# Inverse square roots computed with Newton's iteration on GpSimd instead of ScalarE's Sqrt, and the route exps of a row moved behind the exps of the band

## The chip, the cores and the metric

The kernel runs on one core of one Trainium2 chip. A core has five engines that run their own instruction queues in order and wait for each other through semaphores: TensorE (PE in the profile, with PEld for its weight loads), VectorE (DVE), ScalarE (ACT), GpSimd (POOL) and SyncE (SP, which here issues most of the DMAs). The metric is the device time of one execution in microseconds (us), as the median of several runs.

## The reference, cut to what matters

The program is two transformer-like layers on a float32 input x of shape (4, 512, 128): four batch rows of 512 tokens, 128 channels. In each layer the normalised input goes through an attention and through a mixture of experts, and both results are added to x.

```
def _layernorm(x, axis=-1, eps=1e-05):
    m = jnp.mean(x, axis=axis, keepdims=True)
    v = jnp.var(x, axis=axis, keepdims=True)
    return (x - m) / jnp.sqrt(v + eps)

# layer 0, attention: a window of 64 tokens, 16 heads
strain = disp_win - disp[:, :, :, None, :]
bond_act = gelu(strain @ W_strain + rel_emb @ W_pos)
damage = sigmoid(gelu(strain @ W_dmg + b_dmg) @ W_dmg_out + b_dmg_out)
logits = bond_act @ W_bond - 10.0 * damage
weights = softmax(where(cmask, logits, -inf))
out = einsum(weights, val_win) @ W_cproj

# layer 0, experts: 16, of which 4 are chosen for a token
t = x * rsqrt(mean(x * x, axis=-1) + EPS) * scale
g = einsum('bth,eh->bte', t, gate_w) + gate_b
vals, idx = top_k(g, 4);  w = softmax(vals)
# for each expert: acc + route * (swiglu(t @ w1 + b1) @ w2 + b2)

# layer 1: full attention (16 heads of 8), and 8 relu experts of which 2 are chosen
x = x + _L0_attn_ref(xn, ...) + _L0_ffn_ref(xn, ...)
xn = _layernorm(x)
x = x + _L1_attn_ref(xn, ...) + _L1_ffn_ref(xn, ...)
```

So there are two layernorms for each row, one per layer, and in layer 0 the experts' input t is the layernormed row divided once more by its root mean square. That makes three inverse square roots a row, each on 512 tokens (four tiles of 128, so a 128x4 tile), 12 in all.

## The kernel before

The four rows of the batch are called b = 0 to 3. A row's 512 tokens are four tiles of 128 partitions (TPB = 4). The code is written as Python generators, one for each job, and `weave` (L92) interleaves them: each track gets a number of steps, and the track that is furthest behind issues next. What the generators issue is then ordered by a scheduler that looks at readiness by its own estimates, so the order on an engine is near the woven order, not equal to it.

Jobs of layer 0, for a row b:

- `prepare(b)` (L492), with five yields: the layernorm of the row (xn), its transpose, the four projections `proj`, the division by the root mean square (sq, then tT after a transpose and the scale), the values, the gate scores, and the routes of the 16 experts with `routes` (L238) and `route_rows` (L264). The latter transposes the routes, copies them and stores them to DRAM with a DMA on SP (L275), from where each expert's row is loaded again, broadcast to all partitions (r8, L672).
- `band_logits(b)` (L543): the attention's logits, 64 steps. In each step VectorE subtracts two shifted views of `proj` into a tile z of 128x2048 elements (L560, both inputs in SBUF), ScalarE applies Gelu in place (L562 for the damage half, L566 twice for the bond half), and TensorE reduces z into a PSUM bank (L574). z comes from a pool of four buffers. At the end of the band two subtractions (L616) and two exps (L620) of 128x2048 follow, and their store to DRAM.
- `gated_experts(b)` (L647): the 16 experts, with Relu and Tanh on ScalarE, three instructions on VectorE each, and weights `wT` that are loaded from DRAM into two buffers.
- `band_values(b)` (L304): the weighted values of the attention, through DRAM to turn the band, and the output product.

For layer 1 there are `relu_experts(b)` (L392), which begins with the second layernorm and the routes of the 8 experts and adds up the experts' results on GpSimd (L447), and `full_attention` (L769).

The main loop (L719 to L734) weaves each band in two halves. In the first half the logits run with gated experts of this row, the values of the row before and the relu experts of the row before that. In the second half they run with the rest of the gated experts, with the relu experts of the row before, and with `prepare(b + 1)`, six steps. Row 0 is prepared ahead of the loop. After the fourth band, layer 1's attention runs with the last relu experts woven in.

`layernorm` (L207) takes mean and variance with bn_stats and bn_aggr on VectorE (L212, L215), calls `inv_sqrt` (L223), and forms xn with four instructions on VectorE (L218). `inv_sqrt` is a Sqrt on ScalarE (L226) with eps as bias and a reciprocal on VectorE (L228). For the root mean square VectorE squares the row (L510) and sums it (L512) before `inv_sqrt`. `routes` ranks the scores of a token by comparing all pairs (L248 to L254), takes an exp on ScalarE (L258), and normalises.

ScalarE holds one table of functions at a time. The trace shows an ACT_TABLE_LOAD ahead of the first Sqrt, Gelu or Exp after another of the three; Tanh needs one after Sqrt, and none after Gelu or Exp; Relu, copies and Identity need none.

Of the kernel before, what the change touches and what calls it, by code (L numbers as in the profile page):

```python
# [21 lines left out]

FP = mybir.dt.float32
AF = mybir.ActivationFunctionType
ALU = mybir.AluOpType
AX = mybir.AxisListType
PSUM = bass.MemoryType.PSUM

P = 128
B, T, C = 4, 512, 128  # L30
NT = B * T // P
TPB = T // P
# [59 lines left out]
def weave(*tracks):  # L92
    for _ in woven(*tracks):
        pass
# [3 lines left out]
def two_layers(ctx: ExitStack, tc: tile.TileContext, w: dict, consts: bass.AP, out: bass.AP):  # L98
# [26 lines left out]
    def c_(name):  # L125
        return cst[:, offs[name][0]:offs[name][1]]
# [41 lines left out]
    b2_1 = keep.tile([E1, C], FP, name="b2_1")  # L168
    nc.sync.dma_start(out=b2_1, in_=w["L1_ffn_b2"])

    eps = keep.tile([P, 1], FP, name="eps")
    nc.vector.memset(eps, EPS)
    top = keep.tile([P, 1], FP, name="top")
    nc.vector.memset(top, 0.5 * ALPHA * LIMIT)

# [28 lines left out]
    nc.scalar.copy(posb, pst[:, 0:WIN])  # L204


    def layernorm(b, dst, pin=False):  # L207

        mv = small.tile([P, TPB, 2], FP, tag="mv", name="mv")
        for i in range(TPB):  # L210
            st = small.tile([P, 6], FP, tag="st", name="st")
            ins = nc.vector.bn_stats(st, x1[:, b * TPB + i, :])  # L212
            if pin and not i:
                tc.keep_in_program_order(ins)
            nc.vector.bn_aggr(mv[:, i, :], st)  # L215
        rs = inv_sqrt(mv[:, :, 1], 1.0)
        for i in range(TPB):
            nc.vector.tensor_scalar(  # L218
                dst[:, i, :], x1[:, b * TPB + i, :], mv[:, i, 0:1], rs[:, i:i + 1],
                ALU.subtract, ALU.mult,  # L220
            )

    def inv_sqrt(src, scale):  # L223

        sd = small.tile([P, TPB], FP, tag="sd", name="sd")
        nc.scalar.activation(sd, src, AF.Sqrt, bias=eps, scale=scale)  # L226
        rs = small.tile([P, TPB], FP, tag="rs", name="rs")
        nc.vector.reciprocal(rs, sd)  # L228
        return rs

    def transposed(src):
# [3 lines left out]
            nc.tensor.transpose(pt[:, i * P:(i + 1) * P], src[:, i, :], ident)  # L235
        return pt

    def routes(pool, tag, g, n, k, less, dst):  # L238


        shape = [P, TPB, n, n]
        both = pool.tile([P, 2, TPB, n * n], FP, tag=tag, name="both")
        gt, eq = both[:, 0], both[:, 1]
        other = g[:, :, None, :].to_broadcast(shape)
        own = g[:, :, :, None].to_broadcast(shape)
        gt4 = gt.rearrange("p t (a b) -> p t a b", a=n)
        eq4 = eq.rearrange("p t (a b) -> p t a b", a=n)
        nc.vector.tensor_tensor(gt4, other, own, ALU.is_gt)  # L248
        nc.vector.tensor_tensor(eq4, other, own, ALU.is_equal)
        nc.vector.tensor_tensor(eq, eq, less[:, None, :].to_broadcast([P, TPB, n * n]), ALU.mult)  # L250
        nc.vector.tensor_tensor(gt, gt, eq, ALU.add)
        rank = small.tile([P, TPB, n], FP, tag=f"rank{n}", name="rank")
        nc.vector.tensor_reduce(rank, gt4, AX.X, ALU.add)
        nc.vector.tensor_scalar(rank, rank, float(k), None, ALU.is_lt)  # L254
        mx = small.tile([P, TPB], FP, tag="rmx", name="rmx")
        nc.vector.tensor_reduce(mx, g, AX.X, ALU.max)
        nc.vector.tensor_tensor(dst, g, mx[:, :, None].to_broadcast([P, TPB, n]), ALU.subtract)
        nc.scalar.activation(dst, dst, AF.Exp)  # L258
        nc.vector.tensor_tensor(dst, dst, rank, ALU.mult)
        nc.vector.tensor_reduce(mx, dst, AX.X, ALU.add)  # L260
        nc.vector.reciprocal(mx, mx)
        nc.vector.tensor_tensor(dst, dst, mx[:, :, None].to_broadcast([P, TPB, n]), ALU.mult)
# [195 lines left out]
    with ExitStack() as l0:  # L458
# [29 lines left out]
            nc.scalar.copy(merged[:, :, hg, :], pm[:, 0:2 * P].rearrange("p (k n) -> p k n", k=2))  # L488

        ready = {}  # L490

        def prepare(b):  # L492

            xn = prep.tile([P, TPB, C], FP, tag="xn", name="xn")
            layernorm(b, xn, b > 0)
            pt = transposed(xn)
            xnT = prep.tile([C, T], FP, tag="xnT", name="xnT")
            nc.scalar.copy(xnT, pt)
# [8 lines left out]
            ready[b] = [proj]  # L507
            yield
            sq = prep.tile([P, TPB, C], FP, tag="sq", name="sq")
            nc.vector.tensor_tensor(sq, xn, xn, ALU.mult)  # L510
            ss = small.tile([P, TPB], FP, tag="ss", name="ss")
            nc.vector.tensor_reduce(ss, sq, AX.X, ALU.add)  # L512
            rr = inv_sqrt(ss, 1.0 / C)
            for i in range(TPB):
                nc.vector.tensor_scalar_mul(sq[:, i, :], xn[:, i, :], rr[:, i:i + 1])

# [18 lines left out]
            )  # L535
            yield
            route = small.tile([P, TPB, E0], FP, tag="route0", name="route0")
            routes(zp, "z", scores, E0, K0, c_("lt16"), route)
            rT = route_rows(hold, route, E0, route_d[0][b], LIMIT + 1.0)
            ready[b] += [valn, tT, rT]  # L540
            yield
# [1 line left out]
        def band_logits(b):  # L543
# [70 lines left out]
            for half in range(2):  # L614
                e = zp.tile([P, 4, T], FP, tag="z", name="e")
                nc.vector.tensor_tensor(  # L616
                    e, logits[:, 4 * half:4 * half + 4, :],
                    pt[:, None, :].to_broadcast([P, 4, T]), ALU.subtract,
                )
                nc.scalar.activation(e, e, AF.Exp)  # L620
                nc.sync.dma_start(
                    out=by_t[0:P, 4 * half * T:(4 * half + 4) * T], in_=e.rearrange("p a t -> p (a t)")
                )
# [95 lines left out]
        for b in range(B):  # L719
# [9 lines left out]
            if b > 1:  # L729
                first.append((experts[b - 2], 21))  # L730
            if b + 1 < B:
                second.append((prepare(b + 1), 6))
            weave(*first)
            weave(*second)  # L734


    ctx1 = ctx.enter_context(ExitStack())
# [251 lines left out]
```

## Time and profile before

| what | value |
|---|---|
| median of 3 runs | 1378.02 us (1374.11 to 1379.18) |
| the profiled execution | 1381.3 us, its span 1379.5 us |
| mean granted TensorE clock | 0.941 of full speed |
| L560, subtractions z on VectorE | 256, 554.1 us |
| L562 and L566, Gelu on ScalarE | 128 and 256, 241.4 and 267.3 us |
| ACT_TABLE_LOAD on ScalarE | 43, 1283 ns each |
| Sqrt L226 on ScalarE | 12, 297 to 301 ns |
| reciprocal L228 on VectorE | 12, 164 to 178 ns |
| square L510 and sum L512 on VectorE | 4 each, 684 and 678 ns |
| addition L447 on GpSimd | 32, 1.26 to 9.51 us, median 1.28 |

The span is the time from the first to the last instruction of the profiled execution; the run's time lies 1.8 us above it. Busy times of different engines overlap, so they don't add up to the span. In the views that follow, a group's line gives its count, its busy time, the mean of one in ns, and the idle time of its engine just before it with what ended most of that. A timeline's line gives start and length in us. The order of the changed program's instructions on each engine is known too, without any time.

### The profile page before, as it was taken

How to read it: one execution, taken by the hardware profiler on the slowest of the kernel's cores; microseconds unless marked ns; L12 is line 12 of the kernel's file. 1: busy time of each engine (PE TensorE's matmuls, PEld its weight loads, DVE VectorE, ACT ScalarE, POOL GpSimd, SP SyncE). 2: the span in 40 equal slices, each digit the busy share in tenths (PEclk: the TensorE clock that was granted, in tenths of full speed). 3: DMA queues.
4: the chain of work that ended last, by engine and by line, in shares of the span. 5: the costliest groups of instructions: out<-in, count | busy, mean ns of one | idle time of the engine just before them, and what ended most of it. 6: DMA issues, size and time to landing. Idle time of an engine off the chain costs nothing.

```text
span 1379.5 us, 17426 instructions
## 1 busy us (share of the span) xinstructions
PE 1174.3 (85%) x6763; PEld 450.2 (33%) x6763; DVE 1012.4 (73%) x1085; ACT 1018.5 (74%) x1160; POOL 96.9 (7%) x68
## 2 busy tenths in 40 slices
PE   5676976678889789889989988887999899999997
PEld 2122323123433323353333334232333332333322
DVE  4999998999866999987799998843444434444451
ACT  4899997999968899988889988862454435545554
POOL 2000000000000002200002320012000000000000
PEclk9799998899879999999999999999999989999999
DMA  7121213446212445622244751235133200011100
GB/s 268 44 74 52 76 52 103 100 118 153 62 41 75 150 102 145 170 64 64 73 153 110 180 131 48 67 96 166 49 88 77 69 9 24 24 38 39 31 16 8
DMA packets 168524, 117.61 MB, mean 85 GB/s; under 512 B 66621, under 2 KB 149274, under 8 KB 166906
## 3 DMA queue, kind: packets, MB, share of 16 engines
q1 hardware_dynamic: 166970, 109.77, 29.3%
q0 software_dynamic: 1184, 6.29, 1.2%
q8 instruction: 54, 0.88, 0.3%
q10 hardware_dynamic: 288, 0.43, 0.1%
q14 instruction: 28, 0.23, 0.1%
HBM read 89.00 MB, written 27.46 MB: 84 GB/s over the span
## 4 chain that ended last, share of the span: by engine, by line
PE 59%; ACT 17%; DVE 13%; DMA 6%; issue 5%; SPq 0%; DVEq 0%; ACTq 0%
PE score L920 11%; PE lbank L574 10%; PE bank L381 8%; PE bank L442 7%; ACT z L566 6%; DVE z L560 5%; PE accbank L838 4%; ACT z L562 3%; PE gbank L674 3%; PE accbank L663 3%; DMA wb<-by_s 3%; PE gbank L681 2%; DMA wT<-wT_all 2%; DVE nmax L936 2%; PE abank L810 1%
## 5 line engine op out<-in xcount | busy, mean ns | idle before, releaser
L560 DVE TENSOR_TENSOR z<-proj 128x2044 f32<-128x2044 f32 (+31 forms) x256 | 554.1, 2189 | 29.0 <-PE lbank L574 12.6
L574 PE MATMUL lbank<-z,place 128*32 128x504 f32 (+18 forms) x2048 | 288.9, 639 | 110.1 <-ACT z L566 68.8
L936 DVE TENSOR_REDUCE nmax<-score 128x2 f32<-128x1024 f32 x128 | 156.3, 1225 | 182.3 <-PE score L920 180.1
L566 ACT ACTIVATE z<-z,posb 128x1024 f32<-128x1024 f32 (+31 forms) x256 | 267.3, 1097 | 10.2 <-DVE z L560 8.2
L942 ACT ACTIVATE ex<-score 128x1024 f32<-128x1024 f32 x128 | 130.3, 1023 | 159.7 <-PE score L920 159.7
L562 ACT ACTIVATE z<-z,brep 128x2048 f32<-128x2048 f32 (+31 forms) x128 | 241.4, 1906 | 5.3 <-DVE z L560 4.9
L920 PE MATMUL score<-k,q 32*128 32x512 f32 x512 | 152.2, 655 | 13.9 <-DVE nmax L936 11.7
L447 POOL TENSOR_TENSOR total<-total,part 128x512 f32<-128x512 f32 x32 | 82.6, 2580 | 1038.3 <-DVE part L446 1038.3
L920 PE MATMUL score<-qa,k 32*128 32x512 f32 x512 | 139.7, 648 | 2.1 <-ACT ex L942 2.1
L381 PE MATMUL bank<-xT,ew 128*128 128x512 f32 x256 | 136.2, 626 | 1.6 <-ACT h L389 0.8
L442 PE MATMUL bank<-h,ew 128*128 128x512 f32 x256 | 133.1, 619 | 4.7 <-issue 4.7
L389 ACT ACTIVATE h<-bank,cols 128x512 f32<-128x512 f32 x144 | 97.1, 684 | 45.3 <-PE bank L381 44.6
L574 PEld LDWEIGHTS lbank<-z,place 128*32 128x32 f32 x2048 | 43.0, 112 | 264.2 <-ACT z L566 143.9
L663 PEld LDWEIGHTS accbank<-wT,lin 128*128 128x128 f32 x512 | 72.2, 204 | 60.4 <-issue 34.6
L663 PE MATMUL accbank<-wT,lin 128*128 128x128 f32 x512 | 82.1, 297 | 10.1 <-DVE lin L661 10.1
L674 PE MATMUL gbank<-tT,wT 128*128 128x512 f32 x128 | 72.2, 647 | 17.4 <-DMA wT<-wT_all 16.5
L838 PE MATMUL accbank<-ex,vaug 128*32 128x512 f32 x512 | 70.8, 619 | 0.2 <-ACT ex L942 0.2
L681 PE MATMUL gbank<-tT,wT 128*128 128x512 f32 x128 | 70.6, 635 | 0.0
L920 PEld LDWEIGHTS score<-k,q 32*128 32x128 f32 x512 | 41.2, 187 | 89.0 <-ACT ex L942 44.1
L442 PEld LDWEIGHTS bank<-h,ew 128*128 128x128 f32 x256 | 44.2, 193 | 74.4 <-issue 71.0
L381 PEld LDWEIGHTS bank<-xT,ew 128*128 128x128 f32 x256 | 41.9, 192 | 72.8 <-issue 43.6
L659 DVE SCALAR_TENSOR_TENSOR lin<-lin,r 128x512 f32<-128x512 f32 x64 | 44.5, 695 | 28.6 <-ACT lin L683 28.3
(188 smaller groups left out, 1193.7 us busy)
## 6 DMA issues: line engine op xcount, KB each, us to landing
r<-route SPq DMA_DIRECT2D x96, 256.0 KB, 3.5
ew<-in_L_ffn_W SPq DMA_DIRECT2D x64, 256.0 KB, 3.4
wb<-by_s SPq DMA_DIRECT2D x32, 512.0 KB, 4.1
wT<-wT_all SPq DMA_DIRECT2D x48, 192.0 KB, 3.0
by_t<-e SPq DMA_DIRECT2D x8, 1024.0 KB
f<-by_t SPq DMA_DIRECT2D x128, 64.0 KB, 3.1
by_s<-g SPq DMA_DIRECT2D x16, 512.0 KB, 4.2
wb<-by_s SPq DMA_DIRECT2D x24, 256.0 KB, 3.6
```

Of the source, the lines that this page charges most:

```text
L381: mm = nc.tensor.matmul(ph, wt[:, c * P:(c + 1) * P], xT[:, b * T:(b + 1) * T], start=True, stop=True)
L442: nc.tensor.matmul(py, old[1][:, c, :], old[0][c], start=(c == 0), stop=(c == 3))
L560: nc.vector.tensor_tensor(z[:, :, :, 0:n], seen, own, ALU.subtract)
L562: nc.scalar.activation(z[:, :, :, 0:n], z[:, :, :, 0:n], AF.Gelu, bias=b_dmg)
L566: last = nc.scalar.activation(z[:, dq, :, 0:n], z[:, dq, :, 0:n], AF.Gelu, bias=posb[:, j:j + 1])
L574: mm = nc.tensor.matmul(ps[q:q + 32, t0:T], place[:, kind, 3 - dd:35 - dd], z[:, dq, hg, 0:n], start=(dd == 0), stop=(dd == 3),)
L663: nc.tensor.matmul(ya[:, i * P:(i + 1) * P], lin[:, i * P:(i + 1) * P], wT[:, 2, :], start=False, stop=(e == E0 - 1 and i == TPB - 1),)
L674: nc.tensor.matmul(pg, wT[:, 0, :], tT, start=True, stop=True)
L838: mm = nc.tensor.matmul(av[n][r:r + 32, :], vaug[b % 2][:, i, g * 4 + h, :], ex[n, i][:, h, :], start=(i == 0), stop=(i == TPB - 1),)
L920: mm = nc.tensor.matmul(ps[:, h - two, :], own[r, i * P:(i + 1) * P], seen[r, :], start=True, stop=True)
L936: freed.append(nc.vector.tensor_reduce(nmax[n % 2][:, i, two:two + 2, 8:9], ps, AX.X, ALU.max, negate=True))
L942: freed.append(nc.scalar.activation(ex[n, i][:, two:two + 2, :], ps, AF.Exp, scale=inv))
```

## The change

1. `inv_sqrt` no longer uses ScalarE. It adds eps to the variance, takes a first guess from the float's bits (shift right by one on VectorE, then 0x5F3759DF minus that), and improves it with three Newton steps of four instructions each. All but the shift run on the engine `on`: GpSimd, or VectorE for row 0's layernorm.
2. The root mean square of xn is taken from the variance that the layernorm already has: the mean of xn squared is var times rs squared, two instructions on GpSimd in place of a square and a sum over the row on VectorE.
3. `prepare(b + 1)` gets four steps instead of six in the second half of the band, and what is left of it (the routes and their rows) is issued after that half. The exp of these routes gets a high priority and a dependency without a semaphore that places it behind the band's last exp, `exps[-1]`.

In the changed program the instructions of one inverse root stand on GpSimd as an addition, then, after VectorE's shift, 13 instructions of which each waits for the one before. For the 11 roots that are not row 0's layernorm VectorE's next user (xn or sq) waits for the last of them. In VectorE's order there is nothing between shift and sq for row 0's root mean square and nothing between shift and xn for the last layernorm; elsewhere there are between 2.4 and 4 us of instructions. The routes of rows 1 to 3 stand behind the band's two subtractions for the exps, and their later instructions between the first z of the next band. ScalarE's order holds 17 table loads.

```diff
-    eps = keep.tile([P, 1], FP, name="eps")
-    nc.vector.memset(eps, EPS)
...
-    def layernorm(b, dst, pin=False):
+    def layernorm(b, dst, pin=False, on=nc.gpsimd):
...
-        rs = inv_sqrt(mv[:, :, 1], 1.0)
+        rs = inv_sqrt(mv[:, :, 1], on)
...
+        return mv[:, :, 1], rs
...
-    def inv_sqrt(src, scale):
-        sd = small.tile([P, TPB], FP, tag="sd", name="sd")
-        nc.scalar.activation(sd, src, AF.Sqrt, bias=eps, scale=scale)
+    def inv_sqrt(src, on=nc.gpsimd):
+        v = small.tile([P, TPB], FP, tag="sd", name="sd")
+        on.tensor_scalar(v, src, EPS, None, ALU.add)
+        guess = small.tile([P, TPB], I32, tag="guess", name="guess")
+        nc.vector.tensor_scalar(guess, v.bitcast(I32), 1, None, ALU.logical_shift_right)
         rs = small.tile([P, TPB], FP, tag="rs", name="rs")
-        nc.vector.reciprocal(rs, sd)
+        on.tensor_scalar(rs.bitcast(I32), guess, -1.0, float(0x5F3759DF), ALU.mult, ALU.add)
+        for _ in range(3):
+            a = small.tile([P, TPB], FP, tag="newton", name="newton")
+            on.tensor_tensor(a, rs, rs, ALU.mult)
+            on.tensor_tensor(a, a, v, ALU.mult)
+            on.tensor_scalar(a, a, -0.5, 1.5, ALU.mult, ALU.add)
+            on.tensor_tensor(rs, rs, a, ALU.mult)
         return rs
...
-    def routes(pool, tag, g, n, k, less, dst):
+    def routes(pool, tag, g, n, k, less, dst, behind=None):
...
-        nc.scalar.activation(dst, dst, AF.Exp)
+        with tc.high_priority(offset=4000 if behind else 0):
+            exp = nc.scalar.activation(dst, dst, AF.Exp)
+        if behind:
+            tc.add_manual_dep(
+                exp.ins, behind.ins.name,
+                mybir.DependencyInfo(mybir.DependencyClass.NoSync, mybir.DependencyReason.DATA),
+                reason="one table for both",
+            )
...
-            layernorm(b, xn, b > 0)
+            var, rs = layernorm(b, xn, b > 0, nc.gpsimd if b else nc.vector)
...
-            nc.vector.tensor_tensor(sq, xn, xn, ALU.mult)
-            ss = small.tile([P, TPB], FP, tag="ss", name="ss")
-            nc.vector.tensor_reduce(ss, sq, AX.X, ALU.add)
-            rr = inv_sqrt(ss, 1.0 / C)
+            ms = small.tile([P, TPB], FP, tag="ss", name="ss")
+            nc.gpsimd.tensor_tensor(ms, rs, rs, ALU.mult)
+            nc.gpsimd.tensor_tensor(ms, ms, var, ALU.mult)
+            rr = inv_sqrt(ms)
...
-            routes(zp, "z", scores, E0, K0, c_("lt16"), route)
+            routes(zp, "z", scores, E0, K0, c_("lt16"), route, exps[-1] if exps else None)
...
-                nc.scalar.activation(e, e, AF.Exp)
+                exps.append(nc.scalar.activation(e, e, AF.Exp))
...
-                second.append((prepare(b + 1), 6))
+                preparation = prepare(b + 1)
+                second.append((preparation, 4))
             weave(*first)
             weave(*second)
+            for _ in preparation:
+                pass
```

More of the change, by code (lines that the diff above doesn't have):

```diff
@@ L23 @@
 FP = mybir.dt.float32
+I32 = mybir.dt.int32
 AF = mybir.ActivationFunctionType
@@ L490, in two_layers @@
         ready = {}
+        exps = []
         def prepare(b):
             xn = prep.tile([P, TPB, C], FP, tag="xn", name="xn")
-            layernorm(b, xn, b > 0)
+            var, rs = layernorm(b, xn, b > 0, nc.gpsimd if b else nc.vector)
             pt = transposed(xn)
```

## The prediction

> **What bounds the kernel now.** I read the page first: busy shares and the 40 slices. VectorE (DVE) and ScalarE (ACT) have nearly the same busy time, and both are near nine tenths up to slice 26 (about 900 us), where the last band ends; afterwards PE alone is full.
>
> ```profile
> PE 1174.3 (85%) x6763; PEld 450.2 (33%) x6763; DVE 1012.4 (73%) x1085; ACT 1018.5 (74%) x1160; POOL 96.9 (7%) x68
> DVE  4999998999866999987799998843444434444451
> ACT  4899997999968899988889988862454435545554
> ```
>
> A share over the whole span hides that a band has two halves, so I cut the span at the band ends and at the start of each next row's preparation, and then into shorter stretches (columns after the times: PE, PEld, DVE, ACT, POOL busy with counts, granted clock, DMA).
>
> ```profile
> 133.00:235.00 102.00, 77.18 (x420) 30.92 (x420) 95.52 (x104) 91.12 (x113) 0.11 (x1) 0.88 0.20 61
> 235.00:355.00 120.00, 88.42 (x720) 33.22 (x720) 116.17 (x98) 114.48 (x113) 0.00 (x0) 0.91 0.50 127
> 355.00:470.00 115.00, 102.42 (x422) 43.38 (x423) 84.60 (x119) 90.35 (x109) 4.30 (x4) 0.88 0.24 67
> 600.00:705.00 105.00, 94.72 (x428) 43.23 (x427) 85.37 (x128) 88.14 (x108) 4.19 (x3) 0.95 0.25 75
> ```
>
> ```profile
> 199.00:221.00 22.00, 15.42 (x88) 5.04 (x80) 17.52 (x22) 19.87 (x26) 0.11 (x1) 0.84 0.11 34
> 436.00:456.00 20.00, 16.57 (x76) 7.44 (x75) 18.71 (x24) 16.12 (x21) 1.38 (x2) 1.00 0.30 75
> 671.00:691.00 20.00, 17.15 (x76) 8.15 (x76) 19.68 (x24) 16.45 (x22) 1.70 (x2) 0.91 0.21 66
> ```
>
> First halves (235 to 355) are bound by DVE and ACT together, 97% and 95%. Second halves (355 to 470, 600 to 705) are bound by PE's in-order queue, with ACT only 79 and 84% busy. Inside them one stretch of 20 us belongs to DVE: that of the routes (L248 to L262).
>
> Next, the table loads, by shape, and then those that lie on the chain of waits that ended last (start, length, engine, line; a load has no tile).
>
> ```profile
> L226 ACT ACT_TABLE_LOAD x11 | 14.1, 1283 | 2.0 <-issue 1.8
> L566 ACT ACT_TABLE_LOAD x11 | 14.1, 1283 | 0.2
> L258 ACT ACT_TABLE_LOAD x7 | 9.0, 1283 | 0.1
> ```
>
> ```profile
> 171.10 1.28 ACT L562
> 366.95 1.28 ACT L679
> 610.52 1.28 ACT L566
> 1112.13 1.28 ACT L226
> ```
>
> All seven groups add to 43 loads, 55.2 us of ACT. Only nine are on the chain: these four, and those at 26.98, 232.80, 237.82, 467.55 and 701.82.
>
> Last, GpSimd (POOL), which gets the new work. Its one arithmetic instruction, L447, takes 1.27 us when VectorE runs reductions from PSUM, and 9.50 us when four z subtractions (both inputs in SBUF) run back to back:
>
> ```profile
> 528.40 9.50 POOL L447 TENSOR_TENSOR total<-total,part 128x512 f32<-128x512 f32 x1 [19.49 <-DVE part L446]
> ```
>
> ```profile
> 528.24 8.53 DVE L560 TENSOR_TENSOR z<-proj 128x1976 f32<-128x1976 f32 x4
> ```
>
> **The change, part by part.** All sums are against the profiled span of 1379.5 (its run: 1381.3, 3.3 above the median of 1378.0); I put the difference on the median.
>
> A. *ACT relief.* The changed program's instruction order has 17 table loads: the first (hidden under the input's load, as now), then Gelu, Exp, Gelu in band 0 and four per later band (a pair around each relu route, one Exp and one Gelu at each band's end). 26 fewer x 1.283 = 33.4 us, and 12 square roots x 0.298 = 3.6 us. By place: 6 go in 133 to 235, 9 in 355 to 470, 7 in 600 to 705, 2 in 835 to 930, 2 at 1112. On the chain are the four shown, 5.1 us, and the root at 1113.42, 0.31: **-5.4**. The others (22 loads, 11 roots: 31.5 us) are off it; between 0 and half of that, since 16 of the loads lie in halves where ACT idles 17 to 25 us. Two of PE's waits for a Gelu stand right behind such loads, 5.3 us at 136 and 4.8 at 210; I take half of these, **-5**.
> The row says 1.283 and nothing more: the load at 133.30 starts where the tanh ends (132.64 + 0.64), and its root starts at 134.59. The Trainium skill ("ScalarE: Activation LUTs", What ACT_TABLE_LOAD costs) counts some 2.66 us for a switch, a drain included; 26 would be 69 us, and this trace has no such gap.
>
> B. *Routes of the next row moved behind the band's exps.* What leaves the second half: in the three short stretches the next engine is ACT (19.87 less two loads = 17.3 of 22), PE (16.57 of 20) and PE (17.15 of 20), so at best -4.7 - 3.4 - 2.9 = -11. What comes at the band's end: now from the first subtraction for the exps (L616) to the next band's first Gelu it takes 11.0, 9.7 and 9.7 us (228.08 to 239.12, 464.79 to 474.44, 699.05 to 708.71). After, VectorE has two of these, 4.48, the scores, 0.23, five instructions of the routes before the first z, 4.9 (36.97 to 41.87 in band 0, the same order), and a z, 2.28: 11.9, so +0.9, +2.2, +2.2; and rank (1.21) with five small ones (some 0.2 each) between the next z, in a half where VectorE is 97% busy: +2.2 x 3. Cost 0 to 11.9, taken as 10: **-1**, ends -11 and +12. The moved DMA (L275, the routes' store) goes on SP behind the band's stores and 9 to 13 loads of f; behind it stand the last two f, the r8 loads and wb, which the first expert needs only after its matmul. The weave (6 to 4) also spreads the preparation: by the 32nd z of a band six gated experts have begun instead of five. In 395 to 436 and 640 to 671 PE is 100% busy, and an expert costs it 1.0 + 1.0 + 1.2 = 3.2; in the first half it costs VectorE and ACT 2.1 each: 2 x (2.1 - 3.2) = **-2.2**.
>
> C. *Newton on POOL.* Per inverse root: an addition, a shift on VectorE (which waits for POOL), then 13 dependent POOL instructions on 128x4, then VectorE's xn or sq, which wait; behind these in VectorE's queue are the z, and behind those ACT and PE. On POOL, L447's additions for the experts queue behind. No row shows a 128x4 arithmetic instruction here. Nearest: POOL's memset of 128x16, 0.11 us, below; above, 0.4, a third of L447's 1.27 with its 128 times longer rows. I take 0.2, nearer the small one. While z run, the chain hardly moves (the 9.50), so what VectorE has between is no cover: once it reaches its wait it stands for the chain, 13 x 0.2 = 2.6. Four of the 11 POOL sites are on VectorE's chain:
> - band 0's second root: shift and sq follow each other behind the fourth z (33.8): 2.6 + sq 0.9 + transposes 0.66 + tT 0.67 + L530 1.06 and handoffs give scores at 39.8 instead of 36.64: +3.2;
> - row 1's layernorm at 127 to 140, where the chain is VectorE throughout: 2.6 less three steps gained beside L592: +2.0;
> - the two layernorms at 601 to 606, on VectorE: +2.4;
> - the last one, in attention: 15 steps, 3.2, against 0.64 now (1113.33 to 1113.97): +2.6.
> **+10.2** in all, 54 p - 0.6 for a step of p. The other seven lie where VectorE idles 20 to 30 us per half: 0, at most 2 each. Ends: +5.3 (p = 0.11) and +35 (p = 0.4, and 14).
> What speaks against the change is the Trainium skill ("SBUF — State Buffer", Who interferes with whom): a VectorE instruction with two SBUF inputs and a GpSimd instruction that reads SBUF exclude each other for the whole instruction. With a z of 2.19 before each step a chain would last 28 us, four of them 114; the rows agree on the blocking, but VectorE's own wait ends it.
>
> D. *RMS from the variance.* L510 (0.68) and L512 (0.68) go, four times; about one and a half of these pairs lie where VectorE is the chain (0.66 at 11.11; row 1): **-2**. Band 0's first root moves onto VectorE, 14 small steps at 6.4 to 9, covered by the wait for w_pos to 9.8; without that cover it would cost 1.5.
>
> Sum: -5.4 - 5 - 1 - 2.2 + 10.2 - 2 = **-5.4**, so 1378.0 - 5.4 = 1372.6, said as 1372.
>
> **Rivals.**
> - *ACT was the limit wherever a load stood.* For it: DVE and ACT are equal in sum, and the loads come in clusters (seven in 355 to 385). Against: ACT idles in those halves. Price: half of the 31.5 us instead of 5, and a step of 0.11: -5.4 - 15.7 - 1 - 2.2 + 5.3 - 2 = -21: 1357.
> - *POOL's chain takes the loads' place.* Slower: the step is 0.4, and half of each hidden stall shows. For it: the 9.50 us, and each step waits for the one before. Against: memsets follow each other within 0.1. -15.6 + 35 = +19: 1397. It decides from 54 p - 0.6 = 15.6, p = 0.3.
> - *The routes don't fit at the band's end.* B at +12: 1385. For it: VectorE 97% busy there. Against: ACT must go through the exps and two loads there anyway.
>
> **How the numbers follow.** Forecast 0.46 (own range 1362 to 1381), ACT 0.24, POOL 0.19, routes 0.11. A measurement tells some 0.5% from no change, 1371.1 to 1384.9. Faster: 0.21 of the forecast and 0.24 = 0.45. Same: 0.25, and 0.02 and 0.03 of the last two = 0.30. Slower: 0.17 + 0.08 = 0.25. The range, 1352 to 1394, leaves out the ends of ACT's and POOL's cases.
>
> **What would show it.** Right: 17 loads; POOL steps of some 0.2 us; VectorE waiting 2 to 3 us for POOL at xn and sq; the stretch of the routes gone from the second half; scores of band 0 near 40. Wrong: steps over 0.3 us or POOL waits in VectorE's list above 30 us; second halves shorter by over 10 us each; a first half longer by over 5 us.

## The result, and the profile after

The changed kernel takes 1399.15 us (median of five runs, 1398.56 to 1400.96), the kernel before in the same session 1378.02 (1374.11 to 1379.18): a ratio of 1.0165, 95% interval 1.0147 to 1.0184. It is slower by some 22 us, where 1372 was forecast with a range to 1394. Its profiled execution has a span of 1396.8 us, 17.3 more than that of before.

The page's busy times, and the slices of the engines that changed:

```profile
PE 1180.0 (84%) x6763; PEld 449.9 (32%) x6763; DVE 1007.3 (72%) x1090; ACT 983.0 (70%) x1122; POOL 161.5 (12%) x230
DVE  4899888999796899979679997873444444445451
ACT  4799796889797699979769996963354425555554
POOL 2000110000301013421001331002000000000000
```

ScalarE has 35 us less to do, VectorE 5 less, and yet the span is longer. So on these two the time went into waiting. POOL has 65 us more, but is busy for only 12%: no engine has become full. PE's busy time is 5.7 us longer for the same 6763 matmuls, at a mean granted clock of 0.930 where before had 0.941; whether that matters is taken up with the iterations below.

The table loads are the 17 that the program's order promised (line, engine, operation, count, busy us, ns of one, idle time before):

```profile
L580 ACT ACT_TABLE_LOAD x5 | 6.4, 1283 | 0.1
L268 ACT ACT_TABLE_LOAD x4 | 5.1, 1283 | 0.1
L638 ACT ACT_TABLE_LOAD x4 | 5.1, 1283 | 0.1
L584 ACT ACT_TABLE_LOAD x3 | 3.8, 1283 | 0.1
L179 ACT ACT_TABLE_LOAD x1 | 1.3, 1283 | 1.7 <-PEq L995 1.7
```

The list of VectorE's waits has a kind that was not there before (who waits, for whom, us in all, times, the longest):

```profile
DVE xn L217 <- POOL rs L237: 21.5, 7, 3.7
DVE sq L533 <- POOL rs L237: 10.0, 3, 3.7
```

Ten waits, 31.5 us. One of them in the timeline, VectorE and POOL together (start, length, and in brackets the idle time before and its releaser):

```profile
414.92 0.16 DVE L229 TENSOR_SCALAR guess<-sd 128x4 int32<-128x4 int32 x1
414.99 0.68 DVE L536 TENSOR_TENSOR x<-x,xn 128x512 f32<-128x512 f32 x1
415.16 0.56 POOL L231 TENSOR_SCALAR rs<-guess 128x4 int32<-128x4 int32 x1 [36.28 <-DVE guess L229]
415.59 2.04 DVE L578 TENSOR_TENSOR z<-proj 128x1820 f32<-128x1820 f32 x1
415.81 1.89 POOL L234 TENSOR_TENSOR newton<-rs 128x4 f32<-128x4 f32 x1
417.77 0.20 POOL L235 TENSOR_TENSOR newton<-newton,sd 128x4 f32<-128x4 f32 x1
418.06 0.19 POOL L236 TENSOR_SCALAR newton<-newton 128x4 f32<-128x4 f32 x1
418.34 0.20 POOL L237 TENSOR_TENSOR rs<-rs,newton 128x4 f32<-128x4 f32 x1
...
420.57 0.20 POOL L237 TENSOR_TENSOR rs<-rs,newton 128x4 f32<-128x4 f32 x1
420.81 0.87 DVE L533 TENSOR_SCALAR sq<-xn,rs 128x128 f32<-128x128 f32 x4 [3.17 <-POOL rs L237]
421.59 2.04 DVE L578 TENSOR_TENSOR z<-proj 128x1816 f32<-128x1816 f32 x1
```

Three things are to be seen. A step is 0.20 us long, but the next one starts 0.28 after it (417.77, 418.06, 418.34). While VectorE's z runs (415.59 to 417.63), POOL gets one step through, which takes 1.89 and ends 0.07 after the z; the step before it (415.16) is stretched in the same way beside VectorE's addition x, to 0.56 us. And then VectorE stands for the rest of the chain, with its next z (421.59) behind sq in its queue.

Last, a band's end, where the routes have been put (VectorE, from the subtraction for the exps to the next band's first z):

```profile
459.57 4.49 DVE L634 TENSOR_TENSOR e<-logits,bank 128x2048 f32<-128x2048 f32 x2 [0.21 <-PE bank L244]
467.92 0.69 DVE L462 TENSOR_TENSOR part<-bank,r 128x512 f32<-128x512 f32 x1 [3.87 <-issue]
470.67 0.22 DVE L550 TENSOR_TENSOR scores<-bank,gate_b 128x64 f32<-128x64 f32 x1 [2.05 <-PE bank L548]
470.92 1.23 DVE L257 TENSOR_TENSOR both<-scores 128x1024 f32<-128x1024 f32 x1
...
475.73 2.28 DVE L578 TENSOR_TENSOR z<-proj 128x2048 f32<-128x2048 f32 x1
```

The scores come 11 us after the first subtraction, and the first z 16. From that subtraction to the next band's first Gelu it takes 14.9, 18.5 and 20.2 us, 53.6 together, against 30.4 before. So after this reading there were two suspects: POOL's chains (31.5 us of waits) and the band's end (23 us longer).

### The profile page after: what moved, and what is told of

It reads as the page before. It is cut to its first block, busy times and chain, and to the rows that moved or that the text cites. A ratio compares the mean times of both kernels' runs of the same rounds, so it can differ in the third digit from the quotient of the medians.

```text
span 1396.8 us, 17551 instructions
## 1 busy us (share of the span) xinstructions
PE 1180.0 (84%) x6763; PEld 449.9 (32%) x6763; DVE 1007.3 (72%) x1090; ACT 983.0 (70%) x1122; POOL 161.5 (12%) x230
## 3 DMA queue, kind: packets, MB, share of 16 engines
q1 hardware_dynamic: 166970, 109.77, 29.4%
## 4 chain that ended last, share of the span: by engine, by line
PE 55%; DVE 18%; ACT 12%; issue 8%; DMA 5%; POOL 2%; SPq 1%; DVEq 0%
PE score L941 10%; PE lbank L592 8%; PE bank L397 8%; DVE z L578 8%; PE bank L458 6%; ACT z L584 4%; PE accbank L859 4%; ACT z L580 3%; PE gbank L692 3%; PE gbank L699 2%; PE accbank L681 2%; DVE nmax L957 2%; DMA wb<-by_s 2%; PE bank L244 1%; PE abank L813 1%
## 5 line engine op out<-in xcount | busy, mean ns | idle before, releaser
L592 PE MATMUL lbank<-z,place 128*32 128x504 f32 (+18 forms) x2048 | 289.8, 640 | 102.2 <-ACT z L580 55.8
L463 POOL TENSOR_TENSOR total<-total,part 128x512 f32<-128x512 f32 x32 | 93.5, 2920 | 712.1 <-DVE part L462 712.1
L692 PE MATMUL gbank<-tT,wT 128*128 128x512 f32 x128 | 76.9, 685 | 8.1 <-DMA wT<-wT_all 8.1
L699 PE MATMUL gbank<-tT,wT 128*128 128x512 f32 x128 | 70.8, 636 | 0.0
L695 ACT ACTIVATE glu<-gbank,gbt 128x512 f32<-128x512 f32 x64 | 43.7, 684 | 23.7 <-PE gbank L692 23.5
```

What stands on the lines that cost most here:

```text
L592: mm = nc.tensor.matmul(ps[q:q + 32, t0:T], place[:, kind, 3 - dd:35 - dd], z[:, dq, hg, 0:n], start=(dd == 0), stop=(dd == 3),)
L692: nc.tensor.matmul(pg, wT[:, 0, :], tT, start=True, stop=True)
```

## The experiments

Times are medians. The experiments were timed in groups, each with its own runs of the kernel before (medians 1375.4 to 1378.0); each ratio is to the kernel before of the same group. Where medians and ratios of two groups give different differences, both are said. A table of progress helps: the start of VectorE's z number n (from 0; 64 of them to a band, 256 in all) in the profiled executions, worked out from the traces, as us later than in the kernel before.

```
n      before   after   one_iter  five_iter  row0_dve  no_sqrt
8        52.1    +4.1      +0.7      +4.7      -6.0      -3.6
64      232.5    +9.8      +2.3     +11.7      -1.7      +2.9
128     469.2    +6.5      -5.6     +16.6      -6.8     -10.9
192     703.4   +15.0      -4.0     +36.1      +1.8     -12.4
255     893.9   +22.4      +2.3     +46.5      +9.4     -14.7
```

### Undoing one part each

Newton on VectorE at every root, the routes still at the band's end:

```diff
-    def inv_sqrt(src, on=nc.gpsimd):
+    def inv_sqrt(src, on=nc.vector):
...
-            nc.gpsimd.tensor_tensor(ms, rs, rs, ALU.mult)
+            nc.vector.tensor_tensor(ms, rs, rs, ALU.mult)
```

> Every root's Newton steps (and the mean square) on VectorE; the routes stay behind the band's exps. Theory POOL (the 31.5 us that VectorE waits for POOL at xn and sq are the loss): VectorE does 14 small steps of some 0.1 to 0.2 itself, 2 to 3 us a root in place of 3.2 to 3.7, and is no longer slowed by anything on POOL: 10 to 20 us less than the changed kernel, 1379 to 1389. Theory END (the loss is the way from the first subtraction for the exps to the next band's first Gelu, 14.9 + 18.5 + 20.2 = 53.6 us after against 30.4 before, 23.2 more): those three transitions stay at 50 us or more, and the time at 1390 or more.

1395.65 us, ratio 1.0131 (1.0096 to 1.0166). Only 3.5 to 4.7 below the changed kernel, with transitions of 52.3 us, so END seemed to hold.

The routes back in the second half, Newton still on POOL:

```diff
-                preparation = prepare(b + 1)
-                second.append((preparation, 4))
+                second.append((prepare(b + 1), 6))
...
-            for _ in preparation:
-                pass
...
-            routes(zp, "z", scores, E0, K0, c_("lt16"), route, exps[-1] if exps else None)
+            routes(zp, "z", scores, E0, K0, c_("lt16"), route)
```

> The routes back in the second half (the preparation spread over six steps, no wait for the band's exps); Newton on POOL and the RMS from the variance stay; 23 table loads. Theory POOL: VectorE's waits for POOL stay near 30 us and the time at 1390 or more. Theory END: transitions back near 30 us, 23 us less, of which the six table loads that come back and the routes' place in the second half take 0 to 10 again: 1376 to 1386.

1405.05 us, ratio 1.0196 (1.0158 to 1.0234): slower still, with transitions of 11.3, 9.7 and 8.5, 29.4 us together, as short as before. VectorE's waits for POOL are 33.1 us. END in its simple form is gone, and POOL's forecast for this run held.

The roots by Sqrt again, the rest of the change kept:

```diff
-        on.tensor_scalar(v, src, EPS, None, ALU.add)
...
+        nc.scalar.activation(sd, src, AF.Sqrt, bias=eps, scale=1.0)
+        nc.vector.reciprocal(rs, sd)
```

> The roots back on ScalarE (Sqrt and VectorE's reciprocal, 38 table loads); routes behind the band's exps and the RMS from the variance stay. Theory POOL: 31.5 us of waits gone, some 10 to 15 of them given back to ScalarE's table loads: 1378 to 1389. Theory END: transitions stay at 50 us or more, the time at 1392 or more.

1402.84 us, ratio 1.0170 (1.0113 to 1.0227), in END's interval; the next experiments show that it was for another reason in part.

Newton on VectorE and the routes back, that is, both of the above:

> Both undone: Newton on VectorE, the routes back in the second half; what is left of the change is roots without a table and the RMS from the variance (23 table loads for 43). Theory POOL: as the first run less a few us, 1375 to 1389. Theory END: below the run with Newton on POOL and the routes back by what VectorE saves, 1368 to 1380, and 20 us or more below the first run.

1390.14 us, ratio 1.0094 (1.0062 to 1.0125). Neither theory: POOL plays no part here, the band's end neither, 20 of the 43 loads are gone, and it is still 14 us slower than before. So Newton's steps seem to cost time on VectorE too (the run with the first guess alone, below, shows it), and POOL's are 15 us dearer (1405 against 1390).

### Each part alone

The loads alone, by leaving the root out:

```diff
-        nc.scalar.activation(sd, src, AF.Sqrt, bias=eps, scale=scale)
+        nc.scalar.activation(sd, src, AF.Identity, bias=eps, scale=scale)
```

> The kernel before with the 12 square roots left out (ScalarE writes variance plus eps with the function Identity, which is in every table; the reciprocal follows): 23 table loads instead of 43, nothing put in their place, routes where they were. This part of the computation is left out. It is the whole of what the change can get from the roots' loads. Theory RELIEF (the loads cost what the forecast said, some 8 of its 10.4 us for these 20 loads, and the loss comes from what replaces them): 1364 to 1372. Rival NOTHING (ScalarE's loads lie in its idle time, the order that the scheduler makes around them matters more): 1373 to 1382. Rival LIMIT (ScalarE was the bound at each load): 1350 to 1360.

1365.21 us, ratio 0.9918 (0.9889 to 0.9948): RELIEF. 20 loads are worth 10 to 11 us, 0.5 each of their 1.283.

The routes' move alone (the diff of the run with the routes back, the other way round, on the kernel before):

> The kernel before with the move of the routes alone: preparation spread over four steps, the routes issued after the second half, their exps behind the band's; the roots by Sqrt and the RMS from the squares as before (some 36 loads). Theory END (the move costs about 23 us at the three transitions and wins back less in the second halves): 1388 to 1400. Rival POOL (the move is worth about nothing, as the forecast's -1 with 7 loads fewer): 1368 to 1380.

1390.21 us, ratio 1.0112 (1.0060 to 1.0164). END's number, 15 us slower than before in spite of seven loads fewer.

Both:

> The last two together: square roots left out (this part of the computation is not done) and the routes moved; 17 table loads as in the changed kernel, no Newton, the RMS from the squares. Theory END: 15 us or more above the run without square roots and with the routes in place, 1380 to 1395. Rival POOL: within 5 us of that run or below, 1360 to 1375; then what the changed kernel loses is Newton's, 25 us or more.

1370.27 us, ratio 0.9962 (0.9928 to 0.9997). This run has the changed kernel's 17 loads and its routes, and no Newton. The changed kernel is 28 us above it (1.0165 - 0.9962 = 0.0203 of 1378); by the two intervals it is 21 to 35 us. With no roots in the way, moving the routes costs about 5 us, hardly more than the runs scatter; beside Sqrt it costs 15, and beside Newton on POOL it gains 4 to 6 (1.0196 to 1.0165, or 1405 to 1399).

The preparation earlier, the routes at the band's end as in the changed kernel:

```diff
-                second.append((preparation, 4))
+                second.append((itertools.islice(preparation, 4), 6))
```

> The changed kernel with the four steps of the next row's preparation at the first four of six places of the second half, as before, instead of the four spread over all of it; the routes stay behind the exps. If the lateness of the preparation (scores at 470.7, 11 us after the first subtraction for the exps) makes the transitions long: scores are ready before the exps, the three transitions fall from 53.6 to 40 to 45 us, the time to 1385 to 1392. If the routes' own 5 us on VectorE and the loads do: transitions of 50 us or more, time within 5 us of 1399.

1397.06 us, ratio 1.0158 (1.0094 to 1.0221), though the transitions are now 9.0, 10.6 and 10.6 us, 30.2 together: the 23 us are gone from the band's end and the time is the same. A likely reason, not measured, is that in the long band's end work was done that otherwise is done in the halves beside it. The forecast here was right in its mechanism (the lateness makes the transitions long) and wrong in its price.

### What a step costs

Fewer steps, in the changed kernel:

```diff
-        for _ in range(3):
+        for _ in range(1):
```

> The changed kernel with one Newton iteration instead of three; two iterations of each root are left out. 8 dependent POOL steps fewer at each root. Theory STEPS (VectorE stands for the whole chain at every site, on the time's path: 10 sites x 8 x 0.28 = 22 us, plus what the slowed steps took): 1372 to 1382, VectorE's waits for POOL down from 31.5 to some 10 us. Rival CROSSING (the cost lies in the order and the two crossings between VectorE and POOL, which stay): 1390 to 1398.

1376.01 us, ratio 0.9981 (0.9958 to 1.0005): 23 to 25 us less for 8 steps at 11 roots, 0.26 to 0.29 a step. Its list of VectorE's waits for POOL:

```profile
DVE xn L217 <- POOL rs L237: 7.2, 7, 1.4
DVE sq L533 <- POOL rs L237: 3.3, 3, 1.4
```

10.5 us instead of 31.5. As much left the time as left the waits. The sites that the prediction put on VectorE's chain (its list of four, of which the third is two layernorms, so five of the ten waits) gave up 10.7 us of waits, the other five 10.3. Had only the first group been on the path, half of the gain would have come off.

More steps, range(5):

> The changed kernel with five iterations instead of three: eight POOL steps more at each root. If each step stands on the time's path at the same price: 1399 + 23 = 1422, 1415 to 1428, and VectorE's waits for POOL up from 31.5 to some 53 us. If a part of the waits is hidden from some length on or there is a threshold: 1400 to 1412, or over 1435.

1428.70 us, ratio 1.0362 (1.0330 to 1.0394): 27 to 30 more, at or just above the upper end of the 1415 to 1428 expected, and the waits up to 55.8:

```profile
DVE xn L217 <- POOL rs L237: 35.3, 7, 5.7
DVE sq L533 <- POOL rs L237: 20.5, 4, 5.9
```

No threshold shows: the price is 0.26 to 0.29 us a step from one iteration to three, and 0.31 to 0.34 from three to five. The eleventh root, row 1's second one, which the z covered with three iterations, comes out as a wait too.

Whether the waits merely went along with the loss, or are it, can be read from VectorE's own time up to the end of the last z (us, worked out from the profiled executions, one of each kernel):

```
                       before  no_sqrt  one_iter   after  five_iter  row0_dve
to the end of z 255     896.0    881.2     898.3   918.4      942.5     905.4
busy                    796.8    796.2     791.2   792.7      792.6     794.8
idle, for POOL            0.0      0.0       9.5    28.3       51.2      24.3
idle, all else           99.2     85.1      97.5    97.3       98.6      86.3
```

From one iteration to three and to five the stretch grows by 20.1 and 24.1 us, the waits for POOL by 18.8 and 22.9, and all other idle time stays within 1.3 us. So the waits were added to the idle time and not taken out of it. This also bears on a rival that no run holds fixed, the granted TensorE clock: it is 0.945 with one iteration, 0.930 with three and 0.923 with five, and PE's busy time for the same matmuls is 1166.1, 1180.0 and 1184.0 us. Had the slower PE made VectorE wait longer for the others, the last row would have grown with it.

The second group can be seen by itself in band 1, from z 64 to z 128, where only three of its waits stand (368, 378 and 421 us). With one iteration these waits are 5.9 us shorter and the stretch 4.6; with five they are 7.4 longer and the stretch 8.2. Place by place the match is not always so good: with five iterations band 0 has 6.6 us more of waits and is 1.9 longer.

The same on VectorE: the run of 1390 (Newton there, routes in place) with range(0), the first guess alone.

> The run with Newton on VectorE and the routes in place (1390), all three iterations left out: each root is its first guess, three small VectorE instructions in place of fifteen, values within some 3 per cent of the true ones; 23 loads. If VectorE's steps cost what they did there (25 us for 13 more of them at 12 sites, 0.16 us each): 1390 - 12 x 12 x 0.16 = 1367, 1362 to 1372. If not the steps but the data or the order made the runs without square roots fast: 1376 to 1390.

1365.12 us, ratio 0.9900 (0.9863 to 0.9936): 25 to 27 us for 144 steps, 0.17 to 0.19 each. VectorE's own steps are 0.16 long and start 0.20 apart, so nearly all of their time shows too.

### The other two places

The squares back (the RMS as before, its root on POOL):

```diff
-            nc.gpsimd.tensor_tensor(ms, rs, rs, ALU.mult)
-            nc.gpsimd.tensor_tensor(ms, ms, var, ALU.mult)
-            rr = inv_sqrt(ms)
+            nc.vector.tensor_tensor(sq, xn, xn, ALU.mult)
...
+            nc.vector.tensor_reduce(ss, sq, AX.X, ALU.add)
+            rr = inv_sqrt(ss, nc.gpsimd, 1.0 / C)
```

> The changed kernel with the RMS from the squares again (two VectorE instructions of 0.68 us, four times), its root still on POOL; 17 loads. If the mean square from the variance costs (the run with Sqrt, routes moved and the mean square on POOL was 12.6 us above the one without it): 1386 to 1394. If it gives the 2 us of the forecast: 1399 to 1404.

1398.78 us, ratio 1.0123 (1.0073 to 1.0173). This lies just below the range for a gain and well above that for a cost. Its runs spread from 1390.6 to 1401.2; by the medians the part costs nothing, by the ratios 6 us. A gain of 2 us is unlikely by the intervals, and not excluded by these four runs.

Row 0's second root on VectorE:

```diff
-            nc.gpsimd.tensor_tensor(ms, rs, rs, ALU.mult)
...
+            on = nc.gpsimd if b else nc.vector
+            on.tensor_tensor(ms, rs, rs, ALU.mult)
...
+            rr = inv_sqrt(ms, on)
```

> The changed kernel with row 0's second root on VectorE too, where VectorE stood idle for 11.98 us ahead of the first z; in the changed kernel the shift waits behind four z. If that place is what band 0 pays: scores of band 0 near 31 instead of 40.7, the eighth z 6 to 8 us earlier, and the time 1390 to 1394. If the later waits swallow it: 1396 to 1400.

1389.49 us, ratio 1.0086 (1.0052 to 1.0119): 10 us back from one root. The reason stands in VectorE's timeline. First the changed kernel:

```profile
11.03 0.69 DVE L536 TENSOR_TENSOR x<-x,xn 128x512 f32<-128x512 f32 x1
23.71 2.29 DVE L578 TENSOR_TENSOR z<-proj 128x2048 f32<-128x2048 f32 x1 [11.98 <-ACT proj L523]
...
33.76 0.16 DVE L229 TENSOR_SCALAR guess<-sd 128x4 int32<-128x4 int32 x1
37.59 0.88 DVE L533 TENSOR_SCALAR sq<-xn,rs 128x128 f32<-128x128 f32 x4 [3.67 <-POOL rs L237]
40.73 0.22 DVE L550 TENSOR_TENSOR scores<-bank,gate_b 128x64 f32<-128x64 f32 x1 [2.27 <-PE bank L548]
```

Then this run:

```profile
14.42 0.16 DVE L237 TENSOR_TENSOR rs<-rs,newton 128x4 f32<-128x4 f32 x1
14.62 0.88 DVE L534 TENSOR_SCALAR sq<-xn,rs 128x128 f32<-128x128 f32 x4
19.87 2.29 DVE L579 TENSOR_TENSOR z<-proj 128x2048 f32<-128x2048 f32 x1 [4.38 <-ACT proj L523]
...
28.61 0.22 DVE L551 TENSOR_TENSOR scores<-bank,gate_b 128x64 f32<-128x64 f32 x1 [1.62 <-PE bank L549]
```

In the changed kernel the shift's input was ready at 11.1, and VectorE idled for 12 us; but the scheduler's order has the shift behind four z. On VectorE the whole root lies in that gap, scores come 12 us earlier, and z number 8 comes 10 us earlier (the table above). Of these 10 us 3.8 are there at the first z already (19.87 against 23.71), part of which may not be the root's: ScalarE's copy of relT, which has no part in it, starts 2.1 us earlier (10.86 against 12.96). In VectorE's account the waits for POOL fall by 4 us and the other idle time by 11. The run with Sqrt and the mean square on POOL had the same order, its reciprocal behind four z: its z number 8 is at +5.9, that of the run with the routes alone at -1.7, which is some 8 of the 13 us between these two.

### Looking for a version below both

If the loads are worth 10 us, a root that costs nothing would give 1365. Four versions on this idea. The first, on the kernel before: the four rows' statistics at the start with two square roots, and the RMS root replaced by its first-order term (two small steps);

```diff
-            rr = inv_sqrt(ss, 1.0 / C)
+            nc.vector.tensor_tensor(rr, rs, rs, ALU.mult)
+            nc.vector.tensor_scalar(rr, rr, 0.5 * EPS, 1.0 - 0.5 * EPS, ALU.mult, ALU.add)
```

> A version meant to beat both, on the kernel before: the statistics of all four rows are taken at the start, where VectorE waits, with two square roots on ScalarE; the RMS root is left to its first-order term, 1 - eps/2 + eps/2 times the square of the inverse deviation (two VectorE steps on 128x4), so four roots and the squares go; four roots (of the relu experts) stay; routes stay in place; 34 loads. The run without any square root was 10 us below before; of its 20 loads 9 go here, and VectorE loses the statistics, squares and sums in three second halves, some 3 us each: 1362 to 1372. Rival (the order around row 1 to 3 gets worse, as in the run with Newton on VectorE): 1375 to 1390.

1380.81 us, ratio 1.0023 (1.0000 to 1.0045). The same without any Sqrt, with the routes in place and with the routes moved:

```diff
+            inv_sqrt(all_mv[:, lo:hi, 1], 1.0, all_rs[:, lo:hi], nc.gpsimd if lo else nc.vector)
...
+            on.scalar_tensor_tensor(rs, a, 1.5, rs, ALU.subtract, ALU.mult)
```

> On the kernel before, no square root at all: row 0's statistics and root on VectorE at the start (9 steps, two iterations), those of rows 1 to 3 in one root of 128x12, its steps on POOL, where nothing waits for it for 100 us; RMS from the first-order term, two steps; the four roots of the relu experts by 9 steps on VectorE; routes in place, 23 loads. If the price of a root is only what VectorE spends on its way (four sites x 9 x 0.2 = 7 us): 1365 + 7 less a few us for the statistics that leave the second halves, 1364 to 1374. Rival (the scheduler's order around it decides, as in the run with roots at the start): 1376 to 1388.

1379.49 us, ratio 1.0022 (1.0001 to 1.0042).

> The same with the routes behind the band's exps, as in the changed kernel; 17 loads. From the run without square roots and with the routes moved, 1370: the same 7 us less a few, 1368 to 1378, and 3 to 8 above the one with the routes in place. Rival: at or above 1380.

1380.42 us, ratio 1.0013 (0.9990 to 1.0036).

And with each root at its old place, in nine VectorE steps:

> As the run with the roots at the start and the routes in place, but each row's statistics and root stay where they were in the kernel before: eight roots of 9 VectorE steps (two iterations), the RMS from the first-order term in two steps, 23 loads. If VectorE's own steps are the price (15 of them at 12 sites cost 25 us, 0.14 us each): 1365 + 8 x 7 x 0.14 = 1373, less some for the squares, 1367 to 1376. If the order decides: 1377 to 1386.

1381.24 us, ratio 1.0033 (1.0011 to 1.0055). All four came out on their rivals' side, at the time of before and not 7 us below it.

A control, whether the 10 us were the loads or that run's order: the run without square roots, with its small step on VectorE.

```diff
-        nc.scalar.activation(sd, src, AF.Sqrt, bias=eps, scale=scale)
+        nc.vector.tensor_scalar(sd, src, scale, EPS, ALU.mult, ALU.add)
```

> The run without square roots (that part of the computation is left out) with its one small step (scale and eps) on VectorE in place of ScalarE: the same values, 23 loads, one VectorE instruction of some 0.17 us more at each of 12 sites, another order. If the relief comes from the loads: 1362 to 1370. If it came from that run's order: 1374 to 1382.

1367.11 us, ratio 0.9945 (0.9923 to 0.9968). With the first-guess run this makes three different orders with 23 loads at 1365 to 1367, so the relief is real where nothing long replaces the roots. Why four versions with true roots and short chains stay 12 to 16 us above it is not settled: 56 VectorE steps more at 0.17 would be 10 of the 14 in the last of them, were nothing saved on the squares; those with the roots taken at the start have fewer steps on the way and are no faster. The order that the scheduler makes differs in all of them, and that wasn't held fixed.

## Why the prediction was wrong

*A, the relief from the loads: right in its sum.* Forecast -10.4 for 26 loads; measured -8 to -12 for 20 (three runs), so some 0.5 us a load. The trace has 1.283 a load and no further gap, and most of that was indeed hidden; how the sum splits into loads on and off the chain was not measured. (Between 355 and 385 us stand nine loads, of which seven go; the rival's "seven in 355 to 385" counts the latter.)

*C, Newton on POOL: the step that failed.* The forecast was +10.2; the changed kernel stands 28 us above the run without roots, with D in it. Two parts of the term were off. The smaller: p was taken as 0.2, the length of a step; the chain advances by 0.28. By the prediction's own 54 p - 0.6 that is 14.5 instead of 10.2. That sum also holds one chain for the two layernorms at 601 to 606, both of which waited; with 13 p more it is 18.2, against 16.3 measured at these five places. The larger: "The other seven lie where VectorE idles 20 to 30 us per half: 0, at most 2 each." (With five places in the list there are six others, not seven.) The waits by place, from VectorE's timeline: 3.67 (row 0), 2.60 (row 1's layernorm), 2.88 and 3.44 (611 and 619) and 3.66 (1133) where the prediction had counted them, 16.3 in all; and 2.89, 2.89, 3.17, 3.16 and 3.16 (368, 378, 421, 662, 857) where it had put nothing, 15.3 in all; one root, row 1's second, makes no wait. The runs with one and five iterations show that the second group counts too: over the bands all of the waits are added to VectorE's idle time, and in band 1, where only this group stands, 4.6 us for 5.9 and 8.2 for 7.4. So the idle time of those halves wasn't time that VectorE could have waited in. The timeline at 421 shows why that can be: the next z stands in the queue behind sq, so a wait there delays the z. That ScalarE's Gelus and then PE are held up by it in turn fits the prediction's own reasoning for its listed sites ("behind these in VectorE's queue are the z, and behind those ACT and PE"), but this chain was not followed through at the others.

The rival that named this mechanism forecast 1397, with a step of 0.4 and half of the hidden stalls. The place was right, the parts were not: the steps were 0.28 and all the stalls showed. That its sum lies within 3 us of the measured time is luck, two errors that cancel; its point of decision, p = 0.3, would have said no.

*Row 0's second root.* Forecast +3.2 with scores at 39.8; scores came at 40.73, 4.1 later than before, and the eighth z 4.1 later too: this item was nearly right. What was missed is the gap of 12 us ahead of the first z, in which the root could have been: some 10 us of the whole time lay in that order, which was known when the prediction was made.

*B, the routes' move: -1 and -2.2 forecast.* Measured +5 where roots are free, +15 beside Sqrt, -4 to -6 beside Newton on POOL. Two of these lie within the forecast's ends (-11 to +12) and the one beside Sqrt does not. As a number of its own the term has no meaning: what the move costs depends on what else is in the program, and why it differs so was not found. The transitions grew by 23 us, more than the +0.9, +2.2 and +2.2 of the forecast, because the preparation, spread over four steps, has its scores only after the exps; that growth, however, was no loss that could be measured: the run that took it away has the same time, to some 10 us by its interval.

*D, the RMS from the variance: -2 forecast.* Undoing it made the kernel no slower: by its four runs the part costs 0 to 6 us, so there was probably nothing, or the sign was wrong.

The measured parts, -5 (loads and routes, 1370 against 1375.5) and +28 (Newton, with D), give +23 where the kernel shows +22; as both are differences to the same run, that is no check. VectorE's account of the bands gives the loss another way: against before 4.1 us less work, 28.3 us more waits for POOL, 1.9 us less of other idle time, +22.3. The relief that takes 14 us out of that other idle time in the run without roots is missing in the changed kernel, and there (86.3) once row 0's second root is off POOL.

Of the signs listed ahead, 17 loads, steps of 0.2, waits of VectorE at xn and sq (2.6 to 3.7 us) and scores near 40 were seen, and the one against, "POOL waits in VectorE's list above 30 us", with 31.5.

## What to carry to other kernels

Work that an engine with idle time takes over is not hidden by that idle time: ask who waits for its last step, and what stands behind the waiter in its queue; if that is the work that feeds all the others, the waits can count in full, as here over the bands, wherever the engines idle. Price a chain of small dependent instructions by the distance between starts, not by their length, and test it by leaving out or adding links. And a stretch that becomes longer in the trace is a suspect, not a cause: here 23 us could be taken out of the bands' ends without a measurable effect on the time.

## What the runs showed of the hardware

- A dependent POOL step on 128x4 is 0.19 to 0.20 us long and starts 0.28 after the one before, arithmetic and integer alike; VectorE does the same in 0.16 and 0.20.
- While a VectorE subtraction with two SBUF inputs runs, a POOL step lasts until its end: 1.89 us against a z of 2.04, up to 2.01 in the changed kernel. This agrees with the rule that the prediction weighed (the Trainium skill, "SBUF — State Buffer", Who interferes with whom); with VectorE standing at its own wait, it hit two steps of a chain of thirteen in the timeline shown (0.56 us beside the addition x, 1.89 beside the z).
- A table load of 1.283 us was worth some 0.5 us of the kernel's time; in the windows of before where most of those taken out stand (133 to 235, 355 to 470, 600 to 705), ScalarE was 79 to 89% busy.
- In 94 runs of the kernel before, one program, the mean granted TensorE clock lay between 0.931 and 0.947 and the time between 1369.2 and 1385.8 us: by a straight line through them a clock lower by 0.01 goes with some 9 us more. Which of the two leads the other no run here shows.
